# Attention scores of a graph network: seven half-width products for two blocks of givers in place of eight (Strassen's scheme)

## The chip, the cores and the metric

The kernel runs on one core of a Trainium2 chip, as one program. The metric is the device time of one execution in microseconds (us), and the figure that counts is the median over several executions. Before the change three executions took 2318.16, 2332.40 and 2325.49 us, so the median is 2325.49 us.

The core has engines that run side by side, each through its own list of instructions in order: TensorE (in the profile PE for its matrix products and PEld for its loads of weights), VectorE (DVE), ScalarE (ACT), GpSimd (POOL) and SyncE (SP). An instruction may wait for semaphores that other engines or transfers raise, and everything behind it on its engine then waits too. Products land in PSUM, which has eight banks of 128 x 512 float32; DVE and ACT carry them out of it. Transfers (DMA) are issued by SP and POOL.

## What is computed

A graph of N = 2708 nodes with D = 512 features goes through four layers, each followed by a residual sum and a layer norm. Layers 0, 1 and 3 are products with the (sparse, 0/1) adjacency matrix. Layer 2 holds two attention layers, and they are what the change is about:

```python
def _gat_layer(x, W, adj):
    proj = x @ W
    Wh, Ws = jnp.split(proj, 2, axis=-1)
    scores = Wh @ Ws.T
    a = jax.nn.softmax(scores, axis=-1) * adj
    out = a @ Wh
    out = out + x
    return jax.nn.leaky_relu(out, NEG_SLOPE)
...
for l in range(W_stack.shape[0]):
    x = _gat_layer(x, W_stack[l], adj)
```

The scores are a full 2708 x 2708 matrix per attention layer, in float32; the softmax runs over all of it, and only then does the adjacency pick the few entries that are kept.

## The kernel before

**Blocks and chunks.** The nodes are cut into 22 blocks of 128 rows (`NB = 22`; the last, block 21, has 20 rows). Receiving nodes are handled in six chunks of columns, `CH`: four of 512, one of 384 and one of 276. A tile of 128 x 512 float32 is a "page"; all working tiles come from one pool of `PAGES = 82` pages, and a new tile waits until the last user of its page is done, which may be a transfer.

**A layer of attention.** `project_steps` makes, for each chunk k, four tiles `wst[k][c]` of 128 x 512 (one per quarter c of the features): the weights of the scores, with the givers of that chunk along the columns. All 24 stay in pages for the whole layer. `load_moving` loads the four tiles `xs` of the receivers of a chunk, a page each. The scores of one block of 128 givers by one chunk are four products, summed over c in a bank of PSUM (`scores`):

```python
for c in range(DC):
    nc.tensor.matmul(
        ps[:n, :cw],
        wst[c][:, lo : lo + n],
        ch.xt[c][:, :cw],
        start=(c == 0),
        stop=(c == DC - 1),
    )
nc.scalar.copy(s[:n, :cw], ps[:n, :cw])
```

In the profile this is `sp<-xs,wst_sb`, and the copy on ACT `s<-sp`. A float32 product shows as two records of PE and two loads of weights, so a block is eight records. Block 21 is made by `few`: its four short products go to four strips of one bank, and DVE adds them up (`s<-s,sp`). The banks used here are four, taken in turn.

**The walk.** `layer` walks the chunks, and in each chunk the 22 blocks in the order 0, 1, 2, 21, 3, ..., 20 (step n = 0 to 21). An order written out by hand joins to each step the work of other chunks, and every instruction of an engine is kept in the order of this text (class `Ordered`):

- `greatest`: DVE keeps the running maximum over blocks, `top<-top,s`, one step behind.
- At the start of chunk k the maxima of chunk k-1 (`old`) are finished: `shift_rows` after step 1 (PE transposes `tr_top`, DVE reduces), `shift_columns` after step 2 (PE transposes `tr_mx`, ACT copies the shift).
- `soften(old)`, from step 3 on, one and two calls per step in turn, 23 in all: DVE subtracts the shift from a block (`s<-s,shift`), ACT takes the exponential (`ACTIVATE s<-s`), and for the block before, DVE adds it to the sum (`sum<-sum,s`) and multiplies it by the mask (`s<-s,a`); SP stores it to memory (`pairs<-s`).
- `load_masks(old)` at step 0: six transfers bring all masks of the chunk, four blocks to a page.
- `weigh`: for chunk k-2, products of gathered rows (`acc<-g`), as the gathers that POOL issues (`g<-pairs,givers`) are due. A gather may start only when the chunk is wholly softened and stored. When they come is fixed by a clock of the planner (`advance`), not on the chip.
- `end`: DVE finishes each block of receivers (`xr<-acc`, `r<-xr`; in attention layer 1 a sum, statistics and a layer norm too).
- `load_moving` of the next chunk at step 4.

Chunk k of attention layer a is called a/k below: 0/1 is chunk 1 of layer 0. Chunk 0 of a layer has no `old`, and chunk 1 has one but nothing to weigh. After the last chunk other work fills PE (`fill`): the projection of the next attention layer, or early products of layer 3.

**Around it.** `note` and `index` make, during layer 1 and the first attention chunk, the lists of givers that the gathers use, out of a table `feeds` for all blocks; their small tiles have a pool of their own, `lists`. `other_weights` ends the program with a check on one product.

## Time and profile before

| what | value |
|---|---|
| three executions | 2318.16, 2325.49, 2332.40 us |
| profiled execution: span, first to last instruction | 2297.7 us |
| granted TensorE clock, mean over the span | 0.997 |
| chunks 0/0 to 0/5, first to last score product | 760.2 to 1249.8 us |
| chunks 1/0 to 1/5 | 1456.2 to 1940.4 us |
| all score products `sp`, busy on PE | 798.3 us |
| products of gathered rows `acc<-g`, busy on PE | 264.8 us |
| transfers over the span | 486 MB, 212 GB/s |

The profiled execution is one that the recording wraps: its own time is not listed apart from its span, and the median of the three timed ones is 27.8 us above that span. A row of a group gives line, engine, operation, tiles (output, then inputs) with their shapes, the count, busy time in us, the mean duration of one in ns, and the idle time before them. A row of a window gives its limits and length, and then for each engine the busy time and the number of instructions. All instructions of the attention carry the line L71, that of the recording helper, so they are told apart by their tiles.

### The profile page before, as it was taken

The page shows a single profiled execution, that of the slowest core. Times are in us where ns is not written, and L with a number is a line of the kernel's source. Part 1 is how long each engine was busy: PE and PEld are TensorE (multiplying, and loading weights), DVE is VectorE, ACT ScalarE, POOL GpSimd, SP SyncE. Part 2 cuts the span into 40 slices and gives each one's busy share as a digit, 9 for nine tenths or more (in the row PEclk, how much of TensorE's full clock was granted, in tenths as well). Part 3 has the DMA queues.
Part 4 walks back from the last instruction along what each step waited for, and adds up shares of the span by engine and source line. Part 5 has one row for each costly group of instructions (what it writes and reads, how often), then busy time and mean ns, then how long its engine had stood idle before and what let it go on. Part 6 is the DMA issues. An engine that isn't in the chain of part 4 may idle for free.

```text
span 2297.7 us, 25903 instructions
## 1 busy us (share of the span) xinstructions
PE 2269.4 (99%) x8525; PEld 1289.0 (56%) x8525; DVE 1391.5 (61%) x2803; ACT 675.5 (29%) x1354; POOL 705.4 (31%) x822
## 2 busy tenths in 40 slices
PE   9999999999999999999999999999999999899997
PEld 6776876777644444443555444444443555466685
DVE  6777787786553537748667511238769788525523
ACT  7444452322111123223322200113223334342211
POOL 3433431111000001635557540001635467442000
PEclk9999999999999999999999999999999999999999
DMA  9966752223547415858789997405868799963311
GB/s 351 286 188 184 199 168 81 76 81 104 208 184 267 144 25 184 303 191 297 254 311 360 349 412 284 183 8 179 303 218 286 254 322 339 334 217 120 116 51 43
DMA packets 260929, 486.34 MB, mean 212 GB/s; under 512 B 40238, under 2 KB 126950, under 8 KB 260784
## 3 DMA queue, kind: packets, MB, share of 16 engines
q1 hardware_dynamic: 192128, 269.63, 33.6%
q0 software_dynamic: 68656, 214.96, 28.0%
q8 instruction: 69, 1.13, 0.2%
q14 instruction: 76, 0.62, 0.1%
HBM read 307.55 MB, written 176.92 MB: 211 GB/s over the span
## 4 chain that ended last, share of the span: by engine, by line
PE 86%; DMA 6%; DVE 4%; ACT 1%; issue 1%; POOL 1%; SPq 0%; ACTq 0%; POOLq 0%; DVEq 0%
PE sp L71 33%; PE acc L71 30%; PE mm L71 8%; PE z L71 6%; PE wst L71 6%; DMA x<-x 2%; DMA x<-in_x 1%; DMA at<-in_adj_t 1%; DMA g<-pairs,givers 1%; PE mix L71 1%; DMA pairs<-s 1%; POOL xt L71 1%; PE list L71 1%; ACT m L71 1%; PE tr_x2t L71 0%
## 5 line engine op out<-in xcount | busy, mean ns | idle before, releaser
L71 PE MATMUL sp<-xs,wst_sb 128*128 128x512 f32 (+3 forms) x2112 | 798.3, 544 | 0.0
L71 POOL DMA_INDIRECT g<-pairs,givers x510 | 524.2, 1028 | 872.9 <-issue 338.9
L71 PEld LDWEIGHTS sp<-xs,wst_sb 128*128 128x128 f32 (+1 forms) x2112 | 379.7, 186 | 408.4 <-issue 324.8
L71 PE MATMUL acc<-m,xh 128*128 128x512 f32 (+4 forms) x1584 | 566.8, 379 | 6.6 <-ACT m L71 5.1
L71 PE MATMUL acc<-m,xl 128*128 128x512 f32 (+4 forms) x1584 | 549.6, 365 | 2.0 <-DVE xl L71 1.8
L71 PEld LDWEIGHTS acc<-m,xh 128*128 128x128 f32 (+1 forms) x1584 | 288.0, 188 | 70.9 <-issue 21.3
L71 PEld LDWEIGHTS acc<-m,xl 128*128 128x128 f32 (+1 forms) x1584 | 288.3, 188 | 46.3 <-issue 5.3
L71 PE MATMUL acc<-g 128*32 128x512 f32 (+1 forms) x1020 | 264.8, 606 | 4.6 <-DMA g<-pairs,givers 4.0
L71 ACT COPY s<-sp 128x512 f32<-128x512 f32 (+2 forms) x252 | 132.7, 528 | 396.8 <-PE sp L71 395.1
L71 ACT ACTIVATE s<-s 128x512 f32<-128x512 f32 (+3 forms) x264 | 151.6, 580 | 319.8 <-DVE s L71 319.5
L71 DVE TENSOR_TENSOR top<-top,s 128x512 f32<-128x512 f32 (+2 forms) x240 | 149.1, 621 | 156.1 <-ACT s L71 154.5
L71 PE MATMUL mm<-w,ht 128*128 128x512 f32 (+1 forms) x528 | 223.7, 593 | 0.0
L71 ACT CAST m<-at 128x512 fp32r<-128x512 uint8 (+5 forms) x396 | 199.2, 567 | 62.3 <-DMA at<-mask 19.7
L71 DVE TENSOR_TENSOR s<-s,shift 128x512 f32<-128x512 f32 (+3 forms) x264 | 162.7, 620 | 36.2 <-ACT shift L71 36.2
L71 DVE TENSOR_TENSOR s<-s,a 128x512 f32<-128x512 f32 (+3 forms) x264 | 165.8, 628 | 13.6 <-DMA a<-mask 4.5
L71 DVE TENSOR_TENSOR sum<-sum,s 128x512 f32<-128x512 f32 (+4 forms) x252 | 156.5, 621 | 15.4 <-ACT s L71 15.4
L71 PEld LDWEIGHTS mm<-w,ht 128*128 128x128 f32 (+1 forms) x528 | 95.8, 186 | 117.0 <-issue 112.2
L71 PEld LDWEIGHTS acc<-g 128*32 128x32 f32 (+1 forms) x1020 | 74.6, 134 | 148.0 <-issue 116.5
L71 PE MATMUL z<-w,xt 128*128 128x512 f32 (+1 forms) x352 | 151.0, 596 | 0.0
L71 PE MATMUL wst<-xt,mixed 128*128 128x512 f32 (+2 forms) x384 | 150.5, 544 | 0.0
L71 POOL DMA_DIRECT2D x<-o x44 | 26.0, 597 | 329.7 <-DVE o L71 325.4
L71 PEld LDWEIGHTS wst<-xt,mixed 128*128 128x128 f32 x384 | 72.0, 190 | 71.1 <-issue 58.8
(168 smaller groups left out, 1476.7 us busy)
## 6 DMA issues: line engine op xcount, KB each, us to landing
pairs<-z_sb SPq DMA_DIRECT2D x84, 768.0 KB
pairs<-s SPq DMA_DIRECT2D x168, 256.0 KB
at<-in_adj_t SPq DMA_DIRECT2D x84, 256.0 KB
xres<-x POOLq DMA_DIRECT2D x44, 256.0 KB, 4.6
x<-o POOLq DMA_DIRECT2D x43, 256.0 KB, 3.4
pairs<-s SPq DMA_DIRECT2D x84, 128.0 KB
x<-x SPq DMA_DIRECT2D x37, 256.0 KB
at<-mask SPq DMA_DIRECT2D x32, 256.0 KB
```

Source lines behind the costliest of these rows:

```text
L71: ins = call(*args, **kw)
```

## The change

**Seven products for eight.** For a pair of giver blocks and the two halves of a chunk's columns the scores are a 2 x 2 arrangement of halves: the features are split in two (c = 0, 1 and c = 2, 3), the givers in two blocks, the receivers in two half chunks. Written out, that takes eight products of halves; Strassen's scheme (Winograd's form) takes seven, with sums of the operands before and of the results after. Ten pairs of blocks are formed in each chunk (`pairs_of`): two pairs in each of the first four chunks of givers, and one pair in each of the last two. Block 18 (`ALONE`) and block 21 are made as before. Chunks of receivers with 384 columns or more are done this way (`SEVEN`: five of six, with halves of 256 and 192); the last, of 276, as before.

**Sums of weights.** `sum_weights`, called in `project_steps` after the `wst` of each chunk, makes S1, S2 and S4 (six DVE instructions, three more pages per chunk of givers) and stores the quarter a21 to memory. S3 is formed in place of a21 at first use (`replace`, two DVE instructions), and for the last chunk of receivers a21 is brought back by transfers (`restore`).

**Sums of receivers.** `sum_moving` makes T1, T2 and T4 per chunk (six DVE instructions, three pages); T3 takes the place of a half of `xs` (`replace_moving`, two DVE instructions).

**The walk** of such a chunk is a generator: step 0 makes block 18, then each pair takes two steps, and the products 7 and 4 of a pair are issued between those of the next pair. Results leave PSUM in five copies on ACT of half the width, and two DVE instructions complete the blocks of a pair: `first_block`, an addition at full width that reads PSUM, and `second_block`, one of half width. `soften` is spread otherwise (one call in the middle of each step from step 2 on, and one more at every third step) and is three stages deep, with the exponential one call later. Masks come a group of four at a time: `load_mask`, called four softened blocks ahead of their use. `load_moving` of the next chunk moves from step 4 to step 17, `sum_moving` follows at step 20. The rows that `end` adds in layer 1 are fetched later.

**Pages.** There are 87 instead of 82. `feeds` becomes a page per chunk, cleared by POOL, and the small tiles of `index` and `one_hot` become parts of pages; the matrix of ones in `other_weights` is made on the spot.

```diff
-PAGES, WIDES = 82, 11
+PAGES, WIDES = 87, 11
...
+def pairs_of(k):
+    return {4: (1, P), 5: (1, P)}.get(k, (2, 2 * P))
+SOFT = NB + 2
+ALONE = 18
+SEVEN = [k for k in range(len(CH)) if CH[k][1] >= 384]
...
+    def sum_weights(self, ly, k):
...
+        for c in range(2):
+            nc.vector.tensor_add(tiles["s1"][c], a21[c], a22[c])
+            nc.vector.tensor_sub(tiles["s2"][c], tiles["s1"][c], a11[c])
+            nc.vector.tensor_sub(tiles["s4"][c], a12[c], tiles["s2"][c])
+            nc.sync.dma_start(self.quarter[ly.number][k][c], a21[c])
...
+    PRODUCTS = {
+        1: ("a11", "b11"),
+        2: ("a12", "b21"),
+        3: ("s4", "b22"),
+        4: ("a22", "t4"),
+        5: ("s1", "t1"),
+        6: ("s2", "t2"),
+        7: ("s3", "t3"),
+    }
+    def product(self, ch, pair, n, out, start=False):
+        (k, b), (w, x) = pair, self.PRODUCTS[n]
+        for c in range(2):
+            self.nc.tensor.matmul(
+                out,
+                ch.ly.sums[k][w][c][:, bass.ts(b, P)],
+                ch.part[x][c],
...
+        for p in pairs:
+            self.replace(ch.ly, p[0])
+            t = begin(p)
+            self.product(ch, p, 1, t["x"], start=True)
+            nc.scalar.copy(t["s"][:, :h], t["x"])
+            yield "mid"
+            if old:
+                seven(old)
+            t["y"] = self.bank(0, f"spy{t['name']}")
+            self.product(ch, p, 2, t["y"][:, :h], start=True)
+            self.product(ch, p, 5, t["y"][:, h:cw], start=True)
+            nc.scalar.copy(t["r"][:, h:cw], t["y"][:, h:cw])
+            if old:
+                first_block(old)
+            yield "end"
+            if old:
+                four(old)
+            yield "mid"
+            self.product(ch, p, 6, t["x"])
+            nc.scalar.copy(t["s"][:, h:cw], t["x"])
+            self.product(ch, p, 3, t["y"][:, h:cw])
+            if old:
+                second_block(old)
+            old = t
+            yield "end"
...
-    def load_masks(self, ch):
-        for j0, j1 in GROUPS:
-            a = self.page(f"a{ch.name}_{j0}", U8, (P, DC, ch.cw))
...
+    def load_mask(self, ch, g):
+        j0, j1 = g * DC, min((g + 1) * DC, NB)
+        a = self.page(f"a{ch.name}_{j0}", U8, (P, DC, ch.cw))
...
             nc.vector.tensor_sub(s, s, ch.shift[:n, :cw])
+        if 0 < v <= NB:
+            s = ch.s[v - 1][: rows_of(v - 1), :cw]
             nc.scalar.activation(s, s, AF.Exp)
-        j = v - 1
+        j = v - 2
         if j < 0:
             return
+        if j % DC == 0 and j + DC < NB:
+            self.load_mask(ch, j // DC + 1)
...
+            for what in self.walk(ch):
+                if what == "mid":
+                    if old and n >= 2 and old.softened < SOFT:
+                        self.soften(old)
+                    continue
+                n += 1
...
-                    for _ in range(1 + n % 2):
-                        if old.softened <= NB:
+                    for _ in range(n % 3 == 0 if ch.seven else 1 + n % 2):
+                        if old.softened < SOFT:
                             self.soften(old)
...
-                if n == 4 and k + 1 < len(chunks):
-                    self.load_moving(chunks[k + 1])
+                if following and n == 17:
+                    self.load_moving(following)
+                if following and following.seven and n == 20:
+                    self.sum_moving(following)
```

`seven` and `four` issue products 7 and 4 on the bank `x` of a pair and copy it to a page `v` and to the second block; each product is two calls of a half-width matmul, one per half of the split features.

## The prediction

> **What bounds the kernel now.** First the page's span, busy times and chain of waits, then busy time by stage (one window per chunk), then the groups by shape, then the order of time inside chunk 0/1. The page:
>
> ```profile
> span 2297.7 us, 25903 instructions
> PE 2269.4 (99%) x8525; PEld 1289.0 (56%) x8525; DVE 1391.5 (61%) x2803; ACT 675.5 (29%) x1354; POOL 705.4 (31%) x822
> ...
> PE 86%; DMA 6%; DVE 4%; ACT 1%; issue 1%; POOL 1%; SPq 0%; ACTq 0%; POOLq 0%; DVEq 0%
> ```
>
> PE is the bound, score products the largest item. But 61% on DVE is a mean. Windows (limits, length, busy on PE, PEld, DVE, ACT, POOL) of chunks 0/0, 0/1, 0/2, 1/2, 1/4:
>
> ```profile
> 760.20:835.00 74.80, 74.77 (x229) 33.36 (x226) 27.44 (x43) 12.21 (x23) 0.00 (x0) 1.00 0.18 61
> 835.00:909.10 74.10, 74.10 (x185) 32.83 (x184) 58.40 (x93) 26.13 (x45) 4.42 (x4) 1.00 0.37 118
> 909.10:1009.20 100.10, 100.10 (x305) 42.13 (x304) 64.78 (x102) 27.69 (x48) 55.38 (x56) 1.00 0.78 271
> 1603.80:1702.10 98.30, 98.30 (x289) 40.42 (x288) 73.40 (x124) 28.51 (x47) 51.34 (x51) 1.00 0.76 268
> 1800.40:1881.20 80.80, 80.58 (x290) 40.38 (x289) 67.12 (x115) 23.08 (x44) 50.30 (x47) 1.00 0.90 312
> ...
> 845.90:901.80 55.90, 55.90 (x139) 24.54 (x138) 53.22 (x85) 23.20 (x40) 0.00 (x0) 1.00 0.37 118
> ```
>
> The last line is the softening stretch of 0/1: there DVE is busy 53.22 of 55.90 us, as full as PE. Nobody pays for that now, since PE has four banks to run ahead into. Inside it, DVE works back to back:
>
> ```profile
> 862.28 0.68 DVE L71 TENSOR_TENSOR top<-top,s 128x512 f32<-128x512 f32 x1
> 862.89 0.68 DVE L71 TENSOR_TENSOR s<-s,shift 128x512 f32<-128x512 f32 x1
> 863.49 0.68 DVE L71 TENSOR_TENSOR sum<-sum,s 128x512 f32<-128x512 f32 x1
> 864.20 0.69 DVE L71 TENSOR_TENSOR s<-s,a 128x512 f32<-128x512 f32 x1
> 864.81 0.68 DVE L71 TENSOR_TENSOR s<-s,shift 128x512 f32<-128x512 f32 x1
> ...
> 863.60 0.63 ACT L71 ACTIVATE s<-s 128x512 f32<-128x512 f32 x1 [1.43 <-DVE s L71]
> ```
>
> From start to start an operation at full width costs 0.60 us (0.71 where the next one depends on it), so a softened block costs 864.81 - 862.89 = 1.92 us. ACT's exponential waits for DVE, and ACT is also what empties PSUM.
>
> **The change part by part.** *PE.* What a narrower product costs is read from the loads of weights, one per record (start, length, count):
>
> ```profile
> 863.21 0.19 PEld L71 LDWEIGHTS sp<-xs,wst_sb 128*128 128x128 f32 x1 [0.24 <-issue]
> 863.64 0.19 PEld L71 LDWEIGHTS sp<-xs,wst_sb 128*128 128x128 f32 x1 [0.24 <-issue]
> ...
> 1225.15 1.82 PEld L71 LDWEIGHTS sp<-xs,wst_sb 128*128 128x128 f32 x8 [0.24 <-issue]
> ...
> 919.87 0.86 PEld L71 LDWEIGHTS den<-ones,sum 128*128 128x128 f32 x7 [0.24 <-issue]
> ```
>
> 512 columns take 0.43 us per record; 276 columns (1.82 - 0.19) / 7 = 0.233. That is 0.84 ns a column at both widths, with no extra for the narrower. So 256 columns should take 0.216 and 192 columns 0.163; both lie below the narrowest float32 row, so they are bounded from below by loads alone: seven for products one column wide take 0.86, 0.12 each. A load lasts 0.19, longer than 0.163, but loads at 0.12 apart show that they overlap; at worst a 192 record takes 0.19.
>
> A chunk of 512: 20 blocks x 8 records x 0.43 = 68.8 becomes 10 pairs x 28 records x 0.216 = 60.5: -8.3 us. The chunk of 384: 160 x 0.322 = 51.5 becomes 280 x 0.163 = 45.6: -5.9 (at 0.19 it would be 53.2, +1.7). Two layers: 8 x 8.3 + 2 x 5.9 = 78 us off PE.
>
> The Trainium skill (TensorE: Matmul & The Clock Gate, Part 3: Packing small matmuls) says that a load overlaps running products only where the row groups differ, which these full-height loads do not. By that rule the 120 added loads of a chunk would stand bare at 0.19, 23 us a chunk and some 230 in all, and the change would lose 150 us. The rows above have the loads within the products' pace, and the measurement decides.
>
> *DVE, per chunk of 512.* Added: ten `first_block` at 0.60 (sums with PSUM have the same mean, 0.68 against 0.69, as those in SBUF), ten `second_block`, six for T, two for T3. Half width from the rows of 512 (0.60) and 276 (mean 0.44 less the same 0.08 overlap, 0.36) is 0.335: 6.0 + 3.4 + 2.7 = 12.1 us. `greatest` is unchanged. In 384: 10 x 0.47 + 12 x 0.27 = 7.9. Chunk 0 of a layer also has twelve `replace`, 4.0.
>
> *ACT, per chunk.* A pair leaves PSUM in five half-width copies where two full ones did: 5 x 0.36 (by the row of 276 columns, 0.375) for 2 x 0.58, 6 us more per chunk on an engine busy 26 of 74. Products 6, 7, 4 and 3 now wait for such a copy, and PE's queue stands behind them; two or more other products, 1.7 us (1.3 at 192), lie between, against some 0.9 for the end of a product, the copy and the next load. Hidden while ACT is not held; an exponential in front costs 0.54 of that slack, and one that waits for DVE more, which is how PE comes to follow DVE.
>
> *Where this lands.* Softening cannot start before the shift is known: in 0/1 the first subtraction is at 847.0, 12 us into the chunk.
> - Chunks 0/0 and 1/0 (DVE 27 and 19): 27 + 16 is far under 66. Full gain, -8.3 each: -16.6.
> - 0/1 and 1/1: from 847.0 DVE had some 55.4 us to do, now 67.5; 11.5 + 67.5 = 79. PE may lead: product 1 of a pair waits for a bank that `first_block` two pairs back frees, with products 4, 6, 3 (2.6 us) between, so it may end about 3 us ahead. 76 against 74.1: +2 each, +4. The gain is gone here.
> - 0/2 and 0/3: PE 100.1 - 8.3 = 91.8; DVE 12 + 73 = 85. Gathered products fill the middle only, and softening outruns PE on both sides: two calls of 1.92 and half-width sums, about 3.7 per step against 3.0 on PE. I take 1.3 off: -7 each, -14.
> - 1/2 and 1/3: DVE 73.4 + 12.1 = 85.5, so 12 + 82 - 3 = 91 against PE 90.0. -8.3 turns into some -5; another 2 each for pages (below): -6 together.
> - 0/4: DVE 61.1 + 7.9 = 69, PE 74.3; uneven again: -3. 1/4: DVE 75 in 74.9, with the late start: 0.
> - 0/5 and 1/5 are made as before, but with masks four blocks ahead, at 1.5 us a block: +2 each, +4. Nothing covers that in 1/5 (DVE 52.4 of 59.2).
> - `sum_weights` adds 36 x 0.335 = 12 us per layer to DVE in the projections, where DVE has room (42.3 of 57 us in 402 to 460; 53 of 206 between the layers). Hidden; without that cover 24. POOL's clearing of `feeds`, 1.7 us at the start, splits in six; zero, POOL is idle two thirds. Stores and restores of quarters add 6 MB to 486: zero. Boundaries and fill order: +2.
>
> Sum: -16.6 + 4 - 14 - 6 - 3 + 4 + 2 = -29.6 us, so the span goes to 2268. The 27.8 us between it and the median stay: 2325.5 - 29.6 = 2296.
>
> *New waits, no row of their own.* A mask is issued on SP behind the store of the last softened block and used four blocks later, 7.7 us of DVE. SP's landings are not listed; POOL's page-sized ones have medians of 3.4 to 7.1 us (`x<-o` 3.4, `g` 6.1, `xres<-in_x` 7.1), one 9.1. From nothing to 1.5 us per mask; I take nothing at 512 and half a us in 0/5 and 1/5. `load_moving` moves behind some 17 stores and is read by `sum_moving` three steps, 10 us, later: zero, at worst 1 us a chunk; DVE's softening would queue behind it. Working pages are shared more tightly: in the order of instructions of the changed kernel some twenty ACT copies of 1/2 and 1/3 wait for a store issued only 9 to 14 us of PE work before. From zero to 1 us each, 20; I take 4.
>
> **The rivals.**
> - *DVE does not bind*: its work slips past chunk ends, and PE's gain arrives almost whole, -55 to -78: 2248 to 2270. For it: DVE sits idle for some 10 us at each chunk's start. Against it: the 2.6 us lead, and exponentials that hold ACT's copies.
> - *No change to measure*: 1/2 to 1/4 lose all, 0/2 to 0/4 half, and only chunks 0/0 and 1/0 are left: about -15, 2310.
> - *Slower*: masks late. Softening is DVE's stream, and where it binds (0/1, 1/1, 1/2, 1/3, both chunks 4 and 5: 8 passes) a late mask stops DVE, then ACT, then PE. Five masks a pass, 40 in all: the forecast turns to no change at 0.75 us late on average and to 1% slower at 1.35 us; a landing of 9.1, as the worst listed, plus SP's issue would do it: 2350. Against it: masks were waited for once before, 4.5 us.
> - *The products do not come cheaper*: loads stand bare, as under the rule weighed above, from 0.24 per half-width record on. The rows speak against it.
>
> **How the numbers follow.** About 1% (23 us) is what a measurement can tell from no change. The forecast, 2275 to 2312, gets 0.52, four fifths of it below 2302; DVE not binding 0.15; no change 0.18; late masks 0.12; bare loads 0.03. Faster by over 1%: 0.42 + 0.15 = 0.57; within: 0.10 + 0.18 = 0.28; slower: 0.15. The range from 2260, halfway into the first rival, to 2328 leaves out those 0.15 and a little of the first.
>
> **What would show it.** PE's records at 256 columns should start 0.216 apart, and 0.163 at 192; `sp` in all near 720 us. Windows: 0/0 and 1/0 at 66, 0/1 at 76 with DVE over 0.9 of it from 12 us on and PE idle some 9 us `<-ACT s` or `<-DVE s`; 0/2 near 93, 1/2 near 95. DVE should gain 100 to 130 us in all. Wrong if 0/1 is much shorter than 74, if waits for `a<-mask` come to over 10 us, or if half-width records exceed 0.23.

## The result, and the profile after

| | median | lowest to highest | executions |
|---|---|---|---|
| before | 2321.82 us | 2313.95 to 2332.40 | 4 |
| after | 2384.01 us | 2377.17 to 2392.95 | 4 |

A fourth execution of before came with the result. The changed kernel is slower: 1.0261 times the time before, with a 95% interval of 1.0213 to 1.0310. The prediction said 2296 us (2260 to 2328).

The page of after, the execution of 2392.95 us:

```profile
span 2391.1 us, 29254 instructions
PE 2250.5 (94%) x9725; PEld 1523.5 (64%) x9725; DVE 1544.5 (65%) x3180; ACT 723.8 (30%) x1654; POOL 709.0 (30%) x827
...
PE 74%; DVE 12%; issue 5%; DMA 4%; another core or an unknown queue 2%; ACT 2%; POOL 1%; SPq 0%; DVEq 0%; POOLq 0%; ACTq 0%
```

PE was idle for 2297.7 - 2269.4 = 28.3 us before and is idle for 2391.1 - 2250.5 = 140.6 us now. In the chain PE falls from 86% to 74%, and DVE rises from 4% to 12%; "another core or an unknown queue" is new. The windows of after for chunks 0/0, 0/1, 0/2, 1/2, 1/3 and 1/4, and then three short ones inside 0/2; columns as before (limits, length, PE, PEld, DVE, ACT, POOL), with the granted clock, the DMA share and GB/s at the end:

```profile
759.30:828.70 69.40, 67.11 (x348) 55.82 (x345) 45.09 (x88) 19.35 (x53) 0.00 (x0) 1.00 0.16 53
828.70:903.10 74.40, 69.02 (x305) 56.31 (x305) 66.14 (x113) 32.10 (x75) 0.00 (x0) 0.98 0.32 101
903.10:1011.90 108.80, 96.84 (x410) 66.88 (x409) 79.89 (x138) 30.66 (x74) 50.58 (x49) 0.94 0.72 236
1636.80:1741.60 104.80, 94.70 (x410) 64.56 (x409) 84.17 (x146) 31.70 (x76) 52.29 (x49) 0.98 0.76 243
1741.60:1846.00 104.40, 96.02 (x410) 64.54 (x409) 86.47 (x154) 32.96 (x77) 50.16 (x49) 0.98 0.74 249
1846.00:1928.90 82.90, 72.89 (x377) 55.41 (x376) 73.72 (x138) 28.65 (x75) 43.92 (x41) 0.96 0.83 280
917.30:920.70 3.40, 0.00 (x0) 0.00 (x0) 2.58 (x4) 0.39 (x2) 1.42 (x2) 1.00 0.76 234
920.70:924.10 3.40, 2.64 (x6) 2.18 (x7) 1.82 (x4) 1.70 (x5) 0.00 (x0) 0.50 0.14 52
924.10:927.50 3.40, 3.40 (x9) 2.69 (x8) 3.27 (x6) 0.75 (x2) 0.00 (x0) 0.50 0.22 77
```

Chunks without gathers (0/0, 0/1) came out near the forecast of 66 and 76. Chunk 0/2 was to take 93 and took 108.8: PE is idle for 12.0 us of it, and its clock is 0.94, where it was 1.00 before. The three last lines show how one stop is paid twice: PE does nothing for 3.4 us at full clock, and the next two such stretches run at 0.50. A busy PE gets half as much done there: in the timeline four half-width records take 1.70 us (925.04 to 926.74), 0.43 each, where one takes 0.216 at full clock. The trace of after has 117 us of granted half clock, that of before 18.

The groups of PE that lead in its idle time (count, then busy time and mean ns, then the idle time before them and who ended it), `spx<-t,wst_sb` being product 4 and `spx<-xs,wst_sb` products 1 and 7:

```profile
L71 PE MATMUL spx<-xs,wst_sb 128*128 128x256 f32 (+1 forms) x800 | 192.7, 380 | 19.2 <-ACT s L71 15.7
L71 PE MATMUL spx<-t,wst_sb 128*128 128x256 f32 (+1 forms) x400 | 107.8, 394 | 43.4 <-ACT v L71 27.2
```

Product 4 adds onto the half bank out of which ACT must first have copied product 7 (`v<-spx`), and product 7 onto that of product 6 (`s<-spx`). Between them lies the lead of 1.7 us that the prediction held to be enough.

Two stretches of the timeline of after (start, duration, engine, what; in brackets the idle time before it and who ended it), one in 0/3 and one in 1/5:

```profile
1018.81 1.03 PE L71 MATMUL spy<-t,s 128*128 128x256 f32 x4
1019.67 0.60 PE L71 MATMUL tr_top<-ident,top 128*128 128x128 f32 x4
...
1021.19 1.13 PE L71 MATMUL spx<-t,s 128*128 128x256 f32 x4
...
1025.46 0.37 ACT L71 COPY s<-spy 128x256 f32<-128x256 f32 x1 [5.30 <-remote]
1025.89 1.47 PE L71 MATMUL spy<-xs,s 128*128 128x256 f32 x4 [3.57 <-issue]
1026.90 0.69 DVE L71 TENSOR_REDUCE mx<-tr_top 128x4 f32<-128x512 f32 x1 [11.55 <-remote]
...
1981.71 0.43 SPq L71 DMA_DIRECT2D a<-mask  x1
...
1997.07 0.56 DVE L71 TENSOR_TENSOR s<-s,a 128x384 f32<-128x384 f32 x1 [14.24 <-DMA a<-mask]
1998.19 0.52 ACT L71 ACTIVATE s<-s 128x384 f32<-128x384 f32 x1 [14.99 <-DVE s L71]
1999.04 0.83 PE L71 MATMUL sp<-xs,wst_sb 128*128 128x276 f32 x1 [10.63 <-ACT s L71]
```

First stretch: product 5 (`spy<-t,s`) ends at 1019.84 and the transposes at 1020.27; both ends are modelled by the profile. ACT's copy of product 5 and DVE's reduction wait, in the kernel's order, for nothing but these, yet they start at 1025.46 and 1026.90, 5.6 and 6.6 us late. Product 3 (`spy<-xs,s`) adds onto the half bank that the copy reads, and so PE stood for 3.57 us. The trace has the rise of TensorE's semaphore that let both go, 0.02 us before each start, but no product that ended near it, and so the profile puts the waits down to "remote", although there is one core. I call such a start a **late release**. In the trace of after all 34 waits under "remote" (24 of ACT and DVE, 10 of POOL) end with a rise of that semaphore, so they are waits for TensorE; ACT's 264 exponentials, which wait for DVE, all start within 0.1 us of the moment when they could. Of the 100 copies of product 5 in after, the middle one starts 0.04 us after the product's modelled end. Ten start over 1 us after both this end and ACT's work before, and in all ten TensorE's semaphore rises 0.02 us before the start. The trace of before on record has no wait under "remote" at all.

Second stretch: a mask asked for at 1981.71 lets DVE go at 1997.07. ACT's exponential stands behind DVE, the copy of a product behind that exponential, and PE behind the copy, for 10.63 us. That is the slower rival's mechanism. The largest waits of the two kinds in after (engine and what waited, total idle time, times, longest; idle time, so part of a wait under "remote" is no lateness):

```profile
ACT s L71 <- remote: 54.5, 12, 9.7
...
DVE s L71 <- DMA a<-mask: 24.5, 7, 14.2
...
DVE mx L71 <- remote: 11.6, 1, 11.6
```

**Where the time went**, from the profile of before (2297.7) to that of after (2391.1): PE's idle time grew by 112.3 us. Its busy time fell by 18.9, where the prediction took 78 of work away. In the 92 us of half clock up to 2050 PE was busy for 72, which is 36 of work lost, at most 49 with the tail; 10 to 23 us of that difference stay unplaced.

### The profile page after: what moved, and what is told of

Same layout as the page of the kernel before. It is cut to its first block, busy times and chain, and to the rows that moved or that the text cites. A ratio compares the mean times of both kernels' runs of the same rounds, so it can differ in the third digit from the quotient of the medians.

```text
span 2391.1 us, 29254 instructions
## 1 busy us (share of the span) xinstructions
PE 2250.5 (94%) x9725; PEld 1523.5 (64%) x9725; DVE 1544.5 (65%) x3180; ACT 723.8 (30%) x1654; POOL 709.0 (30%) x827
## 4 chain that ended last, share of the span: by engine, by line
PE 74%; DVE 12%; issue 5%; DMA 4%; another core or an unknown queue 2%; ACT 2%; POOL 1%; SPq 0%; DVEq 0%; POOLq 0%; ACTq 0%
PE acc L71 30%; PE spx L71 11%; PE mm L71 8%; PE spy L71 7%; PE wst L71 6%; PE z L71 6%; DVE s L71 4%; PE sp L71 3%; DVE sum L71 2%; DVE top L71 1%; DMA at<-in_adj_t 1%; DMA x<-in_x 1%; POOL g L71 1%; DMA pairs<-s 1%
## 5 line engine op out<-in xcount | busy, mean ns | idle before, releaser
L71 PEld LDWEIGHTS acc<-m,xh 128*128 128x128 f32 (+1 forms) x1584 | 288.3, 188 | 64.2 <-issue 19.2
L71 PE MATMUL acc<-g 128*32 128x512 f32 (+1 forms) x1020 | 280.6, 621 | 11.2 <-DMA g<-pairs,givers 9.5
L71 PE MATMUL spx<-xs,wst_sb 128*128 128x256 f32 (+1 forms) x800 | 192.7, 380 | 19.2 <-ACT s L71 15.7
L71 ACT COPY s<-spx 128x256 f32<-128x256 f32 (+1 forms) x300 | 107.0, 360 | 334.8 <-PE spx L71 219.9
L71 DVE TENSOR_TENSOR s<-s,a 128x512 f32<-128x512 f32 (+3 forms) x264 | 166.0, 629 | 48.5 <-DMA a<-mask 24.5
L71 PEld LDWEIGHTS spx<-xs,wst_sb 128*128 128x128 f32 x800 | 148.8, 195 | 67.8 <-issue 23.3
L71 DVE TENSOR_TENSOR top<-top,s 128x512 f32<-128x512 f32 (+4 forms) x240 | 149.5, 623 | 2.3
L71 PE MATMUL spx<-t,wst_sb 128*128 128x256 f32 (+1 forms) x400 | 107.8, 394 | 43.4 <-ACT v L71 27.2
L71 PE MATMUL sp<-xs,wst_sb 128*128 128x276 f32 (+5 forms) x512 | 131.3, 460 | 12.2 <-ACT s L71 12.1
```

Of the source, the lines that this page charges most:

```text
L71: ins = call(*args, **kw)
```

## The experiments

The question was why seven products, which cost PE what was forecast wherever nothing disturbs it, lost 62 us. The theories: **the short lead** (called L in the expectations): TensorE may run only 1.7 us ahead of ACT, and any late release or held copy now stops it. Against it **something that the change holds or asks for**: pages (H), masks that come too late (the slower rival), or the 153 us of work that DVE gained (D). Later **the releases** themselves (R): that they come late only in certain conditions, and that the loss goes with them. A table of stops in the four chunks 0/2, 0/3, 1/2 and 1/3 (x/2 and x/3 for short) is given at the end of the third group; there PE has gathers, softening and products side by side.

One thing is needed to read the times. The first three groups ran on three chips where before takes 2320 to 2325 us and, in kernels with gathers, about a third of the landings of transfers and 11 to 18% of the engines' own semaphore events are missing from the traces (condition A in the expectations); the fourth and fifth ran on one where before takes 2301 to 2303 and 99% of the landings are there, as in the first profile of before (condition B). So a kernel is compared only with the before of its own group, and its ratio is given with the 95% interval.

### First group: take one part away (before 2323.59 us)

**All but the seven products.** Masks, pages, order of loads and softening as changed, the products as before.

```diff
-SEVEN = [k for k in range(len(CH)) if CH[k][1] >= 384]
+SEVEN = []
...
-        self.sum_weights(ly, k)
+        if SEVEN:
+            self.sum_weights(ly, k)
```

> All score blocks are made by eight products as before; everything else of the change stays (87 pages, masks four blocks ahead, softening in three stages, receivers loaded at step 17), and no sums of weights are made. Theory H (held pages and late masks: in the loaded chunks x/2 to x/5 ACT copies and DVE wait for transfers that have not landed, PE then stops, and a stopped PE is granted half its clock): without the 14 pages of sums and the 3 of T there are hardly any waits for pages, the masks stay late once or twice, so 2325 to 2345 us, clock at least 0.99, waits for a<-mask 5 to 20 us. Rival D (DVE's added sums hold PE): 2315 to 2330, as before, and no waits for masks to speak of. Rival R (the rest of the change is the loss, not the seven products): 2360 or more.

2336.16 us, 1.0053 (1.0032 to 1.0074). Its trace, waits and then the windows of 0/2 and 1/2:

```profile
ACT s L71 <- remote: 37.3, 8, 10.4
```
```profile
908.90:1009.00 100.10, 100.10 (x306) 42.16 (x305) 64.76 (x102) 26.52 (x48) 47.88 (x49) 1.00 0.77 254
1609.40:1709.10 99.70, 98.55 (x289) 40.32 (x288) 73.54 (x124) 27.12 (x47) 48.48 (x47) 1.00 0.75 250
```

ACT has waits under "remote" here too, eight of them and up to 10.4 us long. The longest lies in 1/2: its copy starts at 1681.5, 3.8 us after its block's modelled end, and PE, having four banks to run into, is idle for 1.2 us in the whole chunk. In 1/3 a copy is 3.7 us late, and PE is idle for 0.6. (In 0/2 PE is not idle for one moment, but no wait of ACT there is under "remote".) Late releases alone do not lose the time. The rest of the change costs 12.6 us of its own, mostly in 1/5 (63.4 for 59.2) and behind it.

**Seven products in the first chunk of a layer alone.** The quarter a21 of the last two chunks of givers, one pair each, comes back later than it is used, so some of the scores of chunks x/1 to x/4 are made with S3 in its place.

```diff
-SEVEN = [k for k in range(len(CH)) if CH[k][1] >= 384]
+SEVEN = [0]
```

> Seven products only where receivers are chunk 0 of each layer; all other chunks by eight. Theory H: chunks 0/0 and 1/0 keep what they gained (69 and 66 us against 75 and 73), nothing else differs from the kernel with eight products everywhere, so 10 to 15 us below that one: 2310 to 2335. Rival D says the same of chunks 0/0 and 1/0. Rival R: 2350 or more.

2324.48 us, 1.0001 (0.9978 to 1.0024), 11.7 below the kernel above. Chunk 0/0 took 69.4 and 1/0 66.2, where they took 74.7 and 73.4 there: 12.5. The scheme pays where nothing softens beside it.

**Without the completing additions.** Both additions of a pair are left out, so its two blocks are not complete; PE and ACT do the same work, DVE 6.0 + 3.4 us less a chunk.

```diff
-            nc.vector.tensor_add(t["s"][:, :cw], t["s"][:, :cw], t["y"][:, :cw])
...
-            nc.vector.tensor_add(t["r"][:, h:cw], t["r"][:, h:cw], t["v"][:, :h])
```

> Leaves out the two additions on DVE that complete the blocks of a pair (first_block and second_block), so parts of the scores are missing; the products, the copies and all transfers stay. DVE loses some 9.4 us per chunk of 512. Rival D: the stops of PE and with them the half clock vanish, 2384 falls to 2290 to 2330, stops of PE under 40 us in all. Theory H: only 0/1 and 1/1, where DVE is the chain, gain, about 7 us each; in x/2 to x/4 the waits for transfers stay, stops of PE 80 us or more, clock at most 0.985: 2350 to 2372.

2344.66 us, 1.0079 (1.0052 to 1.0107), between the theories. The windows of 0/1 and 0/2:

```profile
835.00:902.60 67.60, 66.74 (x305) 55.41 (x305) 57.77 (x95) 32.06 (x75) 0.00 (x0) 1.00 0.36 111
902.60:1002.90 100.30, 93.92 (x409) 64.66 (x408) 70.67 (x116) 30.36 (x74) 49.39 (x50) 0.97 0.78 257
```

In 0/1 nearly the whole gain comes back (74.4 to 67.6; PE alone would need 65.8 by the forecast): there DVE is the bound, as forecast. In 0/2 DVE is busy for 70.67 of 100.30 us, 6 us more than in before, and PE still stops for 6.4 and loses its clock. DVE's work is a share of the loss in the loaded chunks and not the root of it.

**Masks eight blocks ahead in place of four.**

```diff
-        if j % DC == 0 and j + DC < NB:
-            self.load_mask(ch, j // DC + 1)
+        if j % DC == 0 and j + 2 * DC < NB:
+            self.load_mask(ch, j // DC + 2)
...
+                    self.load_mask(old, 1)
```

> Masks are loaded eight blocks ahead of their use in place of four, which holds one more page. Theory H: the 24.5 us of waits for a<-mask go, above all the 14 us in 1/5 with the half clock behind it, but waits for pages rise a little: 2350 to 2372. Rival D: 2375 to 2395. A third reading, M (late masks are nearly all of the loss): 2310 to 2335.

2361.35 us, 1.0151 (1.0119 to 1.0183). One wait for a mask of 0.5 us is left in its trace, and 1/5 falls from 74.1 to 64.2. Late masks were worth about 1% of the 2.6% (1.0261 against 1.0151). With no late mask the kernel is still slower, so the rival is right in part and wrong as the sole cause.

### Second group: change the lead (before 2324.88 us)

**Whole products with a short lead.** The first experiment again, but its products of chunks x/0 to x/4 take two banks in turn: PE may be one block ahead, 8 x 0.43 = 3.4 us.

```diff
-        ps = self.bank(0, name)
+        if ch.k == len(CH) - 1:
+            ps = self.bank(0, name)
+        else:
+            if not ch.two:
+                ch.two = [self.bank(0, f"two{ch.name}_{e}") for e in range(2)]
+            ps = ch.two[0]
+            ch.two.reverse()
```

> As rest_only (eight products everywhere), but the scores of chunks x/0 to x/4 use two banks of PSUM in turn in place of four, so that TensorE can be only one block, 3.4 us, ahead of ACT's copies. Theory L (lead: the same waits of ACT for pages and for DVE are there with eight products, 37 us of them in rest_only, but four banks hide them from TensorE; seven products leave only 1.7 us between a product and the one that needs its copy): stops of PE in x/1 to x/4 rise from some 3 us to 20 to 50, stretches at half clock appear there, and the time is 2350 to 2390. Rival (the seven products and their pages are what costs, banks do not matter): 2328 to 2344.

2353.94 us, 1.0133 (1.0077 to 1.0190). The window of 0/2:

```profile
908.40:1009.40 101.00, 100.14 (x306) 42.12 (x305) 64.74 (x102) 26.41 (x48) 48.55 (x49) 1.00 0.77 253
```

The lead theory missed here: 2.0 us of stops in the four loaded chunks and 6.0 in x/1 to x/4, where it has 20 to 50; that the time lies in its range is luck. Late releases are there (a copy in 1/3 starts 5.5 us after its block's modelled end), but gathered products lie between the blocks as well. A lead of 3.4 us, with two copies where the seven products have five, is nearly as good as four banks; what this kernel loses it loses in x/5, between the layers and in the tail.

**Seven products with a longer lead.** The order of products is 1, 3 (of the pair before), 7 (before), 2, 5, 6, 4 (before), so that three half products, 2.6 us, lie between a copy and the product that waits for it; bank y comes from the other set.

```diff
+            if old:
+                three(old)
             yield "mid"
...
-            t["y"] = self.bank(0, f"spy{t['name']}")
+            t["y"] = self.bank(1, f"spy{t['name']}")
...
-            if old:
-                four(old)
-            yield "mid"
             self.product(ch, p, 6, t["x"])
             nc.scalar.copy(t["s"][:, h:cw], t["x"])
-            self.product(ch, p, 3, t["y"][:, h:cw])
+            yield "mid"
             if old:
+                four(old)
```

> As the changed kernel, with the products of two pairs issued in the order 1, 3 of the pair before, 7 of the pair before, 2, 5, 6, 4 of the pair before, and bank y taken from the other half of PSUM: at least three products, 2.6 us, lie between a product and the one that needs its copy, where it was two (1.7). DVE, ACT, pages and transfers do the same work. Theory L: stops of PE (130 us) fall by a third or more and half clock (104 us) with them: 2335 to 2368. Theory H (the stops are as long as the late transfers, however the products are ordered): 2372 to 2390. Rival D: 2372 to 2390.

2355.53 us, 1.0120 (1.0086 to 1.0153). The windows of 0/2 and 1/2:

```profile
904.10:1002.80 98.70, 93.08 (x410) 63.94 (x409) 80.89 (x140) 30.92 (x75) 51.97 (x50) 0.98 0.79 259
1611.20:1708.30 97.10, 91.57 (x409) 62.63 (x407) 82.26 (x143) 30.89 (x75) 50.62 (x50) 1.00 0.81 266
```

0/2 takes 98.7 in place of 108.8 and 1/2 97.1 in place of 104.8, with the same work on every engine. The changed kernel with 83 pages, profiled on the same chip as this one, takes 100.8 and 106.3, and 420 for the four loaded chunks together, where this one takes 387; so a single 0/2 varies, and the sum is the safer reading. With 0.9 us more of lead half the loss of the whole kernel is gone. (The other set of banks for y came with the new order; it was not tried alone.)

**Fewer pages.**

```diff
-PAGES, WIDES = 87, 11
+PAGES, WIDES = 83, 11
```

> As the changed kernel with 83 pages in place of 87. Theory H (waits for pages are a main part): ACT's waits on unlisted transfers rise from 66 us to over 100, and the time to 2400 to 2450. Rival D: 2380 to 2395, as before, since DVE's work is unchanged.

2384.61 us, 1.0277 (1.0214 to 1.0339), within the interval the same as after (1.0261). Four pages less change nothing that can be measured; that pages are short is refuted, and the 4 us set down for them in the prediction were not there.

**Seven products in chunk 0 of the kernel before.** Nothing else of the change but the sums; S3 and T3 have pages of their own, and no quarter is stored.

```diff
+        self.half, self.seven = self.cw // 2, k in [0]
...
+        self.sum_weights(ly, k)
...
+            nc.vector.tensor_sub(tiles["s3"][c], a11[c], a21[c])
```

> The kernel before, with seven products only in chunk 0 of each layer, S3 and T3 in pages of their own (no stores or restores of quarters), and nothing else of the change: 82 pages, all masks loaded at step 0, softening in two stages. All theories: 0/0 at 69 and 1/0 at 66 us, 12.5 us less than before; the sums of weights add 16 us of DVE per layer beside projections, which may cost 0 to 4 us: 2309 to 2316, a ratio of 0.994 to 0.998.

2306.94 us, 0.9933 (0.9906 to 0.9961): 17.9 us below before, 9 to 22 by the interval. The two chunks give 13.5 in its profile (68.7 for 74.7 and 65.9 for 73.4).

### Third group: take the gathers away (before 2320.42 us)

**Before once more**, unchanged.

> The kernel before, unchanged, for a second profile of it: the executions timed beside the others have spans of 2309 to 2339 us at clocks of 0.989 to 0.997, while the first profile has 2297.7 at 0.997. All theories: 2310 to 2335, the difference to the first profile in the tail behind 1/5, with stops of TensorE of 30 to 45 us in all in place of 15 and 10 to 35 us at half clock.

2322.14 us, with a span of 2320.2. Against the first profile of before, chunk 0/5 is 7.7 us longer, the tail 8.9 and the stretch between the layers 2.9; "remote" now ends 19.8 us of ACT's waits for `s`. So the median of before holds some late releases too, and none of them stops PE in the chunks of 512.

**Both kernels without gathers.** The 510 indirect transfers are replaced by clearing the tile, so `acc` sums zeros; all other work stays.

```diff
-        self.nc.gpsimd.indirect_dma_start(
-            out=g[:, :width],
...
+        self.nc.gpsimd.memset(g, 0.0)
```

> The changed kernel without the gathers of the attention: GpSimd fills their tiles with zeros instead, so the weighted sums are not those of the reference; scores, softening, stores and masks stay. Theory G (TensorE has no lead, and what uses it up in the loaded chunks is the traffic of the gathers: releases of ACT and pages that come late beside them): stops of TensorE in x/2 to x/4 fall from 64 us to under 30 and half clock there from 55 to under 20, chunks 0/2 and 0/3 take 90 to 95 us, total 2300 to 2345. Rival D (DVE's work sets the loaded chunks): stops stay over 50 us there, 0/2 and 0/3 over 100, total 2360 to 2385.

> The kernel before with the same omission, as a control: with four banks of lead it had hardly any stops in x/2 to x/4, so there is little to win there; the tail and the stretch between the layers may lose some waits for gathers. Both theories: 2290 to 2320.

After without gathers takes 2262.31 us, 0.9737 (0.9711 to 0.9764) of before, which is even below the range of theory G; before without gathers takes 2292.70, 0.9876 (0.9849 to 0.9903). Between the two kernels the change is now worth -30.4 us, where -29.6 was forecast. By the ratios' ends, 0.9711 / 0.9903 to 0.9764 / 0.9849, it makes the kernel faster by 0.9 to 1.9%. After without gathers, chunks 0/1, 0/2 and 1/2:

```profile
837.30:913.40 76.10, 69.29 (x306) 56.21 (x305) 67.74 (x117) 32.10 (x75) 0.00 (x0) 0.98 0.32 100
913.40:1004.20 90.80, 90.34 (x410) 63.13 (x408) 77.55 (x133) 30.83 (x74) 28.75 (x48) 1.00 0.36 117
1579.20:1671.00 91.80, 90.83 (x410) 62.97 (x409) 84.44 (x148) 32.04 (x76) 28.74 (x48) 1.00 0.36 113
```

Before without gathers, chunk 0/2:

```profile
912.90:1013.00 100.10, 100.10 (x305) 42.13 (x304) 65.17 (x102) 27.69 (x48) 28.62 (x48) 1.00 0.34 113
```

Before is the same with and without them, 100.1; after goes from 108.8 to 90.8. No wait is put down to "remote", and 99% of the landings are in the trace, on a chip where a third of them otherwise is not. What the seven products lose, they lose only beside the gathers and their traffic (the waits for masks fall as well, from 24.5 to 12.5 us).

**Longer lead and early masks together.** The two edits shown above.

> The order of products of more_lead together with the masks eight blocks ahead of masks_early. Theory L: the two remedies act on different stops and add, 28 and 23 us: 2322 to 2345, that is the kernel with eight products everywhere (2336) or a little less. Rival D: DVE still sets it, 2348 to 2362.

2326.72 us, 1.0030 (1.0004 to 1.0056). The remedies add: 1.0261 for after, 1.0151 and 1.0120 with one of them, 1.0030 with both. It is still not faster than before.

PE in chunks x/2 and x/3 together, four chunks, from one profiled execution of each kernel, all but the last on chips and in conditions with late releases; stops are length less busy time, and the last column is time granted at half clock:

| kernel | lead on a bank | stops | half clock |
|---|---|---|---|
| all but the seven products | four banks of whole products | 1.8 us | 0 us |
| whole products, two banks | 3.4 us | 2.0 | 0 |
| seven products, longer lead | 2.6 us | 18.6 | 3.4 |
| the same, early masks | 2.6 us | 14.0 | 6.8 |
| after | 1.7 us | 42.6 | 37.6 |
| after, 83 pages | 1.7 us | 39.2 | 20.4 |
| after, early masks | 1.7 us | 34.3 | 17.0 |
| after without the additions | 1.7 us | 26.7 | 20.4 |
| after without gathers | 1.7 us | 3.9 | 0 |

### Fourth and fifth group: what of the gathers, and a better version (before 2303.44 and 2300.95 us)

**Plain reads in place of gathers.** POOL issues as many transfers of as many bytes, but from fixed rows, so the sums are not those of the graph.

```diff
-        self.nc.gpsimd.indirect_dma_start(
...
+        c0 = (q // 2) * PAIR + first
+        self.nc.gpsimd.dma_start(
+            g[:, :width], ch.ly.pairs[ch.k % 2][20 * P : 21 * P, c0 : c0 + width]
+        )
```

> The changed kernel with each indirect gather replaced by a plain read of the same size (128 rows of block 20, same columns) issued at the same place on GpSimd's queue, so the weighted sums are not those of the reference. Theory T (traffic: 165 MB beside the stores and masks delay what ACT waits for): as the changed kernel, 2360 to 2390, stops of TensorE in x/2 to x/4 over 45 us. Theory I (the indirect issue is what delays): as without gathers, 2262 to 2290, stops there under 20 us and no late releases.

> Plain reads in place of indirect gathers, as before. In condition B as measured there: 2400 to 2420, with some 130 us of waits for a<-mask and no late releases. In condition A: if late releases come from the indirect issue, none are seen here either and the time is 2395 to 2425; if they come from traffic, they add to it: 2425 to 2470.

2412.23 us, 1.0452 (1.0422 to 1.0483), and 2402.96 us, 1.0443 (1.0411 to 1.0475): the slowest of all, and for another reason than the theories had: the first time lies outside both their ranges. From the waits of the first:

```profile
DVE s L71 <- DMA a<-mask: 129.0, 21, 21.6
```

No late release is left, but 21 masks come late, which is the slower rival in full size: 0/4 takes 90.9 us and the stretch between the layers 258.8. The run does not tell whether the indirect form makes releases late, because on this chip after itself has none, as the next run shows.

**After once more**, unchanged, on this chip.

> The changed kernel, unchanged. If this call runs where the kernel before takes some 2320 and a third of the landing records is missing (condition A): 2375 to 2395, as at first. If it runs where before takes some 2303 (condition B): theory R (late releases are most of the loss) 2290 to 2325, stops of TensorE in x/2 to x/4 under 30 us; theory M (masks late and no lead, whatever the releases) 2345 to 2380, waits for a<-mask over 40 us.

2318.10 us, 1.0059 (1.0040 to 1.0077). The page, then windows of 0/2 and 1/5, then its waits for masks:

```profile
span 2316.4 us, 29254 instructions
PE 2233.1 (96%) x9725; PEld 1511.8 (65%) x9725; DVE 1543.0 (67%) x3180; ACT 726.6 (31%) x1654; POOL 712.3 (31%) x827
```
```profile
910.50:1006.00 95.50, 93.63 (x410) 63.57 (x409) 81.02 (x140) 30.84 (x74) 51.87 (x50) 1.00 0.81 270
1864.80:1933.30 68.50, 60.73 (x259) 39.95 (x262) 49.63 (x109) 20.13 (x45) 37.03 (x35) 0.95 0.92 316
```
```profile
DVE s L71 <- DMA a<-mask: 35.5, 9, 12.4
```

The same program, with the same gathers, loses 0.6% here where it lost 2.6% there. No wait is put down to "remote", PE stops for 7.9 us in the four loaded chunks, none of it at half clock, and 0/2 takes 95.5. So most of the 62 us goes with the late releases. The 0.6% that is left does not: 1/5 takes 9.3 us more than in the first profile of before, with 7.8 of stops, the stretch between the layers 13 more and the tail 26 more, 7.5 in each of the two being gathered products that moved there.

**Seven products in four chunks, longer lead, early masks.** Chunk x/4 goes back to whole products; a21 comes back one chunk earlier.

```diff
-SEVEN = [k for k in range(len(CH)) if CH[k][1] >= 384]
+SEVEN = [0, 1, 2, 3]
...
-                if following and not following.seven and n >= 7 and n % 4 == 3:
+                if ch.seven and not following.seven and n >= 7 and n % 4 == 3:
...
-                if not following and n == 1:
+                if not ch.seven and n == 1:
```

> As lead_and_masks, with seven products for chunks x/0 to x/3 only; x/4 is made by eight products, so its weighting keeps its place. Theory L: x/4 and the stretches behind it win back 10 us in layer 0 and 12 in layer 1, the rest stays: 2300 to 2316, a ratio to the kernel before of 0.992 to 0.998. If the tail behind 1/5 is as long as in lead_and_masks (some 24 us over the first profile of before), 2316 to 2328.

> Seven products for x/0 to x/3, more lead, masks eight blocks ahead. Condition B: ratio 0.988 to 0.993 to the kernel before, as measured. Condition A: late releases come on top, 2296 to 2316, ratio 0.990 to 0.998.

2283.17 us, 0.9904 (0.9883 to 0.9924), and 2284.29 us, 0.9926 (0.9897 to 0.9954). Chunk 0/2 of the first:

```profile
910.20:1002.20 92.00, 90.49 (x410) 63.01 (x408) 81.01 (x140) 31.38 (x75) 51.51 (x50) 1.00 0.83 277
```

With gathers beside it PE is idle for 1.5 of 92.0 us. This version is 1.0 and 0.7% below before, with both intervals below 1, and ran only on this chip.

**Seven products in chunk 0 of the kernel before**, again.

> The kernel before with seven products in chunk 0 of each layer only. Condition A: as measured, 0.991 to 0.996. Condition B: 12.5 us less than before there, 2288 to 2294, 0.993 to 0.997, so a little more than four_chunks.

2293.34 us, 0.9948 (0.9929 to 0.9966). This small version is 0.5 to 0.7% below before on both kinds of chip, with both intervals below 1.

## Why the prediction was wrong

- **The price of the products: right.** Eight loads of weights at 256 columns, and eight at 192, in the timeline of after:

```profile
777.07 1.70 PEld L71 LDWEIGHTS spx<-xs,wst_sb 128*128 128x128 f32 x8
...
1142.90 1.33 PEld L71 LDWEIGHTS spx<-xs,wst_sb 128*128 128x128 f32 x8
```

(1.70 - 0.19) / 7 = 0.216 and (1.33 - 0.19) / 7 = 0.163, the forecast values. These loads do not stand bare, although at 0.19 each lasts longer than a record's pace at 192; the rule that the prediction weighed does not hold for them. `sp` in all, forecast near 720 us, was busy for 758 in after, with the half clock in it, and for 732 in after once more (798.3 before). The rivals of bare loads and of DVE not binding both fell.

- **Chunks without gathers: right but for 0/0.** 0/0 69.4 (66 forecast; 2.3 us of stops, which the forecast did not have), 1/0 66.2 (66), 0/1 74.4 and 1/1 74.7 (76). DVE binds in x/1, as shown by leaving the additions out. "DVE should gain 100 to 130 us" was too low: it gained 153.0.
- **The sum with nothing beside it: right in total, by chunk only roughly.** Without gathers, by the two profiles: 0/2 -9.3 and 0/3 -7.5 (forecast -7 each), 1/2 and 1/3 together -11.7 (-6), 0/5 and 1/5 -0.8 together (+4). Some 7.5 us of gathered products moved out of each of 0/4 and 1/4 (32 records of `acc<-g` at 0.24); set aside, 0/4 is -1.4 (-3), 1/4 +5.3 (0), and what lies outside the chunks +13, 10 of it in the tail (+2). The two profiles differ by 23.8 in all, the medians by 30.4; misses of both signs cancel, so that the medians come within 1 us of the forecast 29.6 is in part luck.
- **"Hidden while ACT is not held": this step failed.** It set "two or more other products, 1.7 us" against the 0.9 of a product's end, copy and next load, and named only exponentials as what could hold ACT. Beside the gathers TensorE's results reached ACT and DVE up to 5 to 7 us late. Four banks cover that (1.8 us of stops, with all else as changed); 1.7 us did not (42.6), 2.6 did by half (18.6). The 0.9 us is what such a wait typically takes, and the margin was never set against the worst one. The profile of before has no late release, and PE never waits in its windows with gathers, so the worst wait could not be read there; it should have been bounded by more than zero.
- **A stop was priced at its own length: failed.** The granted clock was 0.997 before, and the prediction has no term for it. All clock steps of before and after lie on a grid of 3.413 us. In these two traces every window at full clock in which PE was busy for 0.45 of it or less was followed by one at half clock (19 cases). Of the windows of 0.46 to 0.80 one, of 0.51, was followed by half clock too, and the others were not. Full clock came back only after windows of 0.90 or more. In nine other traces, read in the same way, the border lies between 0.45 and 0.56. The Trainium skill (TensorE: Matmul & The Clock Gate, Part 1: The HAM clock gate) has the free-running window of 3413 ns, and half clock after at least one idle window; the traces agree with the window's length, and differ in that PE need not be idle for all of it.
- **"From nothing to 1.5 us per mask; I take nothing at 512 and half a us" in x/5: too small.** Waits for masks were 24.5 us in after (10 had been named as the sign of being wrong), up to 14.2 for one, and 1/5 took 74.1 us for 59.2 with +2 forecast. Early masks gave back about 1%. The slower rival thus had the sign, and for this part the mechanism; the rest of the loss, which early masks left (2361.35 us), is not in it.
- **"The 27.8 us between it and the median stay": wrong.** An execution's time is its span plus 1.9 us (2392.95 and 2391.1). The first profile of before was an execution of about 2300 us, of the kind that the last two groups have; 27.8 was a difference between conditions and not something around the span. The middle of the forecast is the median less 29.6 either way, so this did not move it; but it hid that executions differ, and that the one that was read had no late release.
- **Pages (4 us)**: nothing, as 83 pages show. **0/4 and 1/4** (-3 and 0): 86.7 and 82.9 in after for 80.2 and 80.8, although 7.5 us of products moved out of each. Without late releases (after once more) they take 71.9 and 76.1, so that with those 7.5 set aside the narrow chunks gain 0.8 and lose 2.9.

What stays open: what makes the releases late. They go with the gathers and with the chip, and where they occur the trace also lacks landings. Within the traces they follow runs of gathers: all 24 of ACT and DVE in after, 15 in the first experiment and 10 in before once more come when POOL has issued at least four gathers in the 8 us before, which holds for 54 to 56% of the time from the first gather to the last. The same runs of gathers make none late in after once more. Whether the indirect form, the bytes, or the recording that every timed execution carries is behind it was not settled: plain reads ran only on the chip where after has no late release either. Nor do the traces tell whether the product itself or only its signal is late, since the ends of products are modelled.

## What to carry to other kernels

The distance between a product and the engine that must empty its bank is a resource like a page: a scheme that saves products by chaining them on fewer banks spends it, and it must be priced against the worst wait in a loaded stretch, not against the mean. In before and after a 3.4 us window in which TensorE was busy for 0.45 or less was always followed by at least one at half clock, so a stop of some 2 us can cost half of the next window as well. Put such a scheme first where the other engines idle (chunk 0 of each layer gave 0.5 to 0.7% with no other change), and lengthen the lead and the masks' notice before going on.

## What the runs showed of the hardware

- Waits of ACT and DVE for TensorE that end up to 5 to 7 us after the product's modelled end, beside gathers on the chips of the first three groups and in none of the four profiles with gathers on the chip of the last two; the same program took 1.0261 of before where they occur and 1.0059 where they do not.
- Half clock after 3.413 us windows that are only partly idle (busy for 0.45 or less, 19 cases in before and after), for 3.4 us or more at 0.50.
- As many plain reads as there were gathers were followed by far longer waits for masks (129.0 and 120.9 us against 35.5 on the same chip).
